# A transformer block with attention and expert choice: the first tiles reordered, the first expert's tokens in two halves

## The chip, the core and the metric

The kernel runs on one NeuronCore of a Trainium2 chip. The core has five engines with their own instruction streams: TensorE (PE: matrix products, results in PSUM), VectorE (DVE), ScalarE (ACT), GpSimd (POOL) and SyncE (SP, which here only issues DMAs). An engine works through its own stream in order and waits for others by semaphores. The metric is the device time of one execution in microseconds (us); smaller is better.

## The reference

One block on x of 8 batches with 1024 tokens of 256 numbers each, all in float32. First attention with 16 heads of 64, then a feed-forward layer in which each of 8 experts chooses its 512 best tokens of all 8192:

```python
mod = (silu(c) @ wmod).reshape(8, 6, 1, 256)      # sa, ca, ga, sb, cb, gb
h = layernorm(x) * (1 + ca) + sa
x = x + ga * attention(h, w_qkv, w_o)             # 16 heads, softmax over 1024 keys
h = layernorm(x) * (1 + cb) + sb
scores = softmax(h @ router_w + router_b)
G, idx = top_k(scores.T, 512)                     # per expert
h1 = relu(h[idx] @ w1 + b1)                       # 256 -> 1024
eo = h1 @ w2 + b2                                 # 1024 -> 256
y = zeros.at[idx].add(eo * G)
x = x + gb * y
```

(ga and gb are kept at least 0.25 away from zero.)

## The kernel before

**Order.** Everything of note lies under a manual schedule: what the Python code emits first stands first in its engine's stream. Tiles, banks of PSUM and semaphores are managed by the framework: an instruction waits until what it reads is written, and until the buffer that it writes is free.

**Beginning.** `first_loads` queues the loads on SP: part of wmod, x of batch 0 as four tiles `x_first` of 256 tokens (tiles 0 and 1; then the k and q weights of the first four heads, in this order; then tiles 2 and 3), then the v weights. `mod_silu` and `mod_columns` make modT (shift and 1 + scale, by columns); its two copies out of PSUM are VectorE's (L218, L219). For each tile, `ln_first` takes mean and variance (L116, L117, VectorE), `ln_norm` has GpSimd make 1/std (`rstd_of`, L106 and L108) and VectorE normalize in place (L288), and `ln_out` turns the tile by four transposes into one PSUM bank (L301) and evicts it to hT with modT as scale and bias, both of its halves k=0 and k=1 on ScalarE (L305). The order is: statistics 0, statistics 1, norm 0, modT, statistics 2, norm 1, statistics 3, norm 2, norm 3.

**Attention.** The loop over g follows. A unit u is one batch, one pair of heads and 512 queries; it takes four steps of g, each with two tiles of 128 keys. A step multiplies scores (L375), copies them to SBUF (L384, ScalarE) and takes the running maximum (L389, VectorE); the maximum is then subtracted (L437, VectorE), exp taken (L440, ScalarE), the values multiplied (L450) and the sums of exp added up on GpSimd (L470, L473). Other work is put between by hand: `at(g, where, f, ...)` appends f to a list that step g runs at its place "m1", "m2", "load", "post" or "pool". Step -1 runs before all scores. There stand `ln_out` of tiles 0 and 1, then `qk_task` i=0 (k of tokens 0 to 511) and i=2 (q of the same tokens, L340, evicted by L347 and L345). Step 0 runs two tiles of scores, then `ln_out` of tiles 2 and 3, then `qk_task` i=1 (k of tokens 512 to 1023). Step 1 has the next scores, `qk_task` i=3, and the first `v_task`. Banks of PSUM for this early work come from the list `early`, one bank each in the order of use.

**Output and router.** `out_proj` and what follows put each batch's tokens, with their expert scores, into a table rows_d in DRAM; the last batch is done after the loop. A search on VectorE and TensorE finds each expert's threshold, and a scan gives each chosen token its slot, split into lo (5 bits) and hi.

**Experts.** `entries(e)` builds one-hot matrices on VectorE: hot (32 wide, L1132), at_hi (16 wide, L1137), and ids, which is at_hi times the token number's two parts (L1142, L1145). `choose(e)` multiplies them (L1156), `gather(e)` folds the result to 512 token numbers and has GpSimd gather the rows, 128 per DMA (L1180). `turn(e)` transposes four row tiles twice (k=0, 1; L1193) into two banks and VectorE copies them to xT (L1196). `inner(e, f)`, f=0..7, multiplies by w1 (L1204, three PSUM banks in turn) and ScalarE applies relu with the bias (L1208). `outer(e, j)`, j=0..3, multiplies by w2 (L1216), VectorE adds the bias and multiplies by the gates (L1221, L1222) and GpSimd scatters with addition to the output (L1225), each scatter behind the one before. `entries(e+1)` is emitted ahead of `inner(e)`, `choose(e+1)` and `gather(e+1)` behind its f=4 and f=5, `turn(e+1)` behind `outer(e, 2)`. For expert 0 all of entries, choose, gather and turn lie bare. The last expert runs its inner and outer for two halves of 256 tokens.

Of the kernel before, what the change touches and what calls it, by code (L numbers as in the profile page):

```python
# [28 lines left out]
F32 = mybir.dt.float32  # L29
BF16 = mybir.dt.bfloat16  # L30
# [3 lines left out]
AF = mybir.ActivationFunctionType  # L34
ALU = mybir.AluOpType
# [4 lines left out]
P = 128  # L40
# [4 lines left out]
def adaln_block(  # L45
# [15 lines left out]
    nc = tc.nc  # L61
    B, S, D = x.shape
    H, _, _, N = w_qkv.shape
    E, _, F = w1.shape
    K = 512
# [143 lines left out]
    def mod_columns():  # L209

        pm = ps_av.tile([P, 2 * KC, B], F32, tag="av", name="pm")
        for m in range(2 * KC):
            for k in range(KC):
                nc.tensor.matmul(
                    pm[:, m, :], wm[0][:, k, m * P : (m + 1) * P], sT[:, k, :],
                    start=(k == 0), stop=(k == KC - 1),
                )
        nc.vector.tensor_copy(modT[:, :KC, :], pm[:, :KC, :])  # L218
        nc.vector.tensor_scalar_add(modT[:, KC:, :], pm[:, KC:, :], 1.0)  # L219

    def mod_rows(i):

# [28 lines left out]
    def at(g, where, f, *args):  # L251
        steps.setdefault((g, where), []).append((f, args))
# [40 lines left out]
    def ln_out(b, t):  # L293
        if t == 0:
            hTs[b] = work.tile([P, KC, S], F32, tag="hT", name=f"hT{b}")
        xt = ln_x.pop((b, t))[0]
        pt = bank([P, KC, 2 * P], f"ptx{b}_{t}")
        if b == 0:
            for k in range(KC):
                for i in range(2):  # L300
                    nc.tensor.transpose(  # L301
                        pt[:, k, i * P : (i + 1) * P], xt[:, i, k * P : (k + 1) * P], ident
                    )
            for k in range(KC):
                nc.scalar.activation(  # L305
                    hTs[b][:, k, 2 * t * P : (2 * t + 2) * P], pt[:, k, :], AF.Identity,
                    bias=modT[:, k, b : b + 1], scale=modT[:, KC + k, b : b + 1],
                )
# [23 lines left out]
    def qk_task(b, p, i):  # L332
        a, half = (1, i) if i < 2 else (0, i - 2)
        if half == 0:
            qks[b, p, a] = work.tile([P, S], F32, tag="qk"[a], name=f"qk{a}_{b}_{p}")
        pq = bank([P, 512], f"pq{b}_{p}_{i}")
        sl = slice(half * 512, half * 512 + 512)
        for k in range(KC):
            for m in range(2):
                nc.tensor.matmul(  # L340
                    pq[m * N : (m + 1) * N, :], wq_of(k, a, 2 * p + m), hTs[b][:, k, sl],
                    start=(k == 0), stop=(k == KC - 1),
                )
        if a == 0:
            nc.scalar.mul(qks[b, p, a][:, sl], pq, scale)  # L345
        else:
            nc.scalar.copy(qks[b, p, a][:, sl], pq)  # L347

# [382 lines left out]


    for t in range(NT // 2):
        at(-1 if t < 2 else 0, "m1", ln_out, 0, t)
        ln_task(1, t, free_slot(39 + 4 * t, True))
    for i, g in ((0, -1), (2, -1), (1, 0), (3, 1)):
        at(g, "m1", qk_task, 0, 0, i)
    for t, g in enumerate((1, 2, 3)):
        at(g, "m1", v_task, 0, 0, t)
    for b in range(B):  # L740
# [48 lines left out]
    with tc.manual_schedule():  # L789
# [4 lines left out]
        ln_first(1)  # L794
        ln_norm(0, 0)
        mod_columns()
        for t in range(2, NT // 2):
            ln_first(t)
            ln_norm(0, t - 1)
        ln_norm(0, NT // 2 - 1)  # L800
        for t in parts_of:
            nc.vector.memset(t, 0.0)
        g = -1
# [96 lines left out]
        def turn(t):  # L900
            out_turn(ps_m, b, t, tag="mm")
# [226 lines left out]
    def entries(e):  # L1128


        hot = ew.tile([P, KT, C, LO], BF16, tag="hot", name=f"hot{e}")
        nc.vector.tensor_tensor(  # L1132
            hot, iota_lo.unsqueeze(1).unsqueeze(1).to_broadcast([P, KT, C, LO]),
            lo[:, :, e, :].unsqueeze(3).to_broadcast([P, KT, C, LO]), ALU.is_equal,
        )
        at_hi = ew.tile([P, KT, C, HI], BF16, tag="at_hi", name=f"at_hi{e}")
        nc.vector.tensor_tensor(  # L1137
            at_hi, hi[:, :, e, :].unsqueeze(3).to_broadcast([P, KT, C, HI]),
            iota_hi.unsqueeze(1).unsqueeze(1).to_broadcast([P, KT, C, HI]), ALU.is_equal,
        )  # L1140
        ids = ew.tile([P, KT, C, 2 * HI], BF16, tag="ids", name=f"ids{e}")
        nc.vector.tensor_tensor(  # L1142
            ids[:, :, :, :HI], at_hi, first.unsqueeze(3).to_broadcast([P, KT, C, HI]), ALU.mult
        )
        nc.vector.tensor_scalar(ids[:, :, :, HI:], at_hi, part, None, op0=ALU.mult)  # L1145
        chosen[e] = hot, ids

    def choose(e):
# [35 lines left out]
            rows.append(row)  # L1184
        chosen[e] = tok, rows

    def turn(e):
        tok, rows = chosen[e]
        xT = ew.tile([P, KC, K], F32, tag="xT", name=f"xT{e}")
        for k in range(KC):  # L1190
            px = ps_x.tile([P, K], F32, tag="px", name=f"px{e}_{k}")
            for j in range(KT):
                nc.tensor.transpose(  # L1193
                    px[:, j * P : (j + 1) * P], rows[j][:, k * P : (k + 1) * P], ident
                )
            nc.vector.tensor_copy(xT[:, k, :], px)  # L1196
        h1 = ew.tile([P, FC, K], F32, tag="h1", name=f"h1_{e}")
        chosen[e] = tok, rows, xT, h1

    def inner(e, f, t0=0, n=K):  # L1200
        tok, rows, xT, h1 = chosen[e]
# [31 lines left out]
    with tc.manual_schedule():  # L1233
        entries(0)
        choose(0)
        gather(0)
        turn(0)
        for e in range(E - 1):
            entries(e + 1)
            for f in range(FC):  # L1240
                inner(e, f)
                if f == FC // 2:
                    choose(e + 1)
                if f == FC // 2 + 1:
# [12 lines left out]


# [29 lines left out]
```

## Time and profile before

| What | Value |
|---|---|
| Median of 3 runs (lowest, highest) | 3532.61 us (3531.13, 3533.65) |
| The profiled execution's own time | 3532.22 us |
| Its span, first to last instruction | 3530.5 us |
| Mean granted TensorE clock | 0.989 |
| Busy share: PE, DVE, ACT, POOL | 98%, 79%, 69%, 75% |
| First projections of q and k begin | 12.82 us |
| First scores begin | 19.70 us |
| First expert's one-hots begin | 3266.87 us |
| First expert's w1 matmuls begin | 3283.59 us |
| Second expert's w1 matmuls begin | 3315.37 us |

A row of the timeline has start and duration in us, engine, line, operation, the tile written and the tiles read, the shapes and a count; in brackets stands the idle time of the engine before it and what ended it. "128*64" ahead of a shape is the part of TensorE's array in use. A float32 product is two instructions in the rows, and two products on the halves of the array run beside each other. Times given below for single instructions within a row come from the same trace.

### The profile page before, as it was taken

The numbers are of one execution on the slowest core, as the hardware profiler recorded it, in microseconds if no ns is written. First come the engines' busy times: TensorE is split into PE (matmuls) and PEld (weight loads), VectorE is DVE, ScalarE is ACT, GpSimd is POOL, SyncE is SP. The second block draws the span as 40 slices with busy tenths as digits, with TensorE's granted clock in tenths as the row PEclk, the third lists the DMA queues.
The fourth block names the chain that finished last, engine by engine and source line by source line (L and its number), as shares of the span: only waits on it lengthen the run. The fifth ranks groups of instructions, "written<-read, shape, count | busy, mean of one in ns | idle before, by whom it ended". The sixth has DMA issues, their size and how long they took to land. (4 is left out here: it accounts for less than half of the span.)

```text
span 3530.5 us, 54857 instructions
## 1 busy us (share of the span) xinstructions
PE 3444.8 (98%) x20991; PEld 1454.9 (41%) x20991; DVE 2796.1 (79%) x3507; ACT 2438.1 (69%) x2998; POOL 2664.6 (75%) x1555
## 2 busy tenths in 40 slices
PE   8999999999999999999999999999999999996898
PEld 3333334334433434344333444334333434334566
DVE  6888888888888888888888888888888888886332
ACT  5887877777777777777777777777778777770111
POOL 3788777978788887978788887988788887882233
PEclk9999999999999999999999999999999999997899
DMA  4020012111211112111211112111221112124342
GB/s 79 13 43 31 25 46 62 29 40 46 63 48 36 49 54 57 34 40 46 64 48 36 45 58 57 34 40 46 62 50 33 47 58 54 40 77 145 96 103 43
DMA packets 184091, 183.34 MB, mean 52 GB/s; under 512 B 49148, under 2 KB 161292, under 8 KB 183700
## 3 DMA queue, kind: packets, MB, share of 16 engines
q1 hardware_dynamic: 167860, 158.44, 16.1%
q0 software_dynamic: 7168, 12.72, 1.8%
q10 hardware_dynamic: 8800, 8.68, 0.8%
q8 instruction: 165, 2.70, 0.3%
q14 instruction: 98, 0.80, 0.1%
HBM read 126.01 MB, written 62.16 MB: 53 GB/s over the span
## 5 line engine op out<-in xcount | busy, mean ns | idle before, releaser
L473 POOL TENSOR_TENSOR acc<-acc,p 128x1024 f32<-128x1024 f32 x764 | 1811.7, 2371 | 351.9 <-ACT p L440 318.6
L384 ACT COPY p<-s 128x1024 f32<-128x1024 f32 x1024 | 994.6, 1018 | 401.9 <-PE s L375 390.6
L437 DVE TENSOR_TENSOR p<-p,less 128x1024 f32<-128x1024 f32 x1024 | 1205.8, 1209 | 28.5 <-PE less L434 25.8
L389 DVE TENSOR_TENSOR top<-top,s 128x1024 f32<-128x1024 f32 x768 | 936.2, 1219 | 269.1 <-ACT p L384 228.1
L440 ACT ACTIVATE p<-p 128x1024 f32<-128x1024 f32 x1024 | 1041.6, 1057 | 73.4 <-DVE p L437 72.5
L375 PE MATMUL s<-qk,qk 64*128 64x512 f32 x4096 | 1020.3, 611 | 15.0 <-DVE parts L415 12.0
L450 PE MATMUL av<-p,v 128*64 128x512 f32 x4096 | 970.0, 593 | 1.6 <-ACT p L440 1.6
L375 PEld LDWEIGHTS s<-qk,qk 64*128 64x128 f32 x4096 | 359.2, 186 | 512.4 <-issue 221.5
L340 PE MATMUL pq<-hT,wq 128*64 128x512 f32 x2048 | 498.0, 607 | 2.2 <-ACT hT L305 2.2
L450 PEld LDWEIGHTS av<-p,v 128*64 128x64 f32 x4096 | 279.3, 137 | 457.4 <-issue 353.5
L470 POOL TENSOR_TENSOR acc<-p,p 128x1024 f32<-128x1024 f32 x128 | 304.0, 2375 | 163.9 <-ACT p L440 163.9
L340 PEld LDWEIGHTS pq<-hT,wq 128*64 128x64 f32 x2048 | 125.1, 136 | 341.5 <-issue 205.5
L357 PE MATMUL pv<-wq,hT 128*64 128x256 f32 x2048 | 249.2, 385 | 0.0
L591 PE MATMUL po<-wo,ot 128*64 128x256 f32 x1792 | 205.7, 382 | 0.0
L357 PEld LDWEIGHTS pv<-wq,hT 128*64 128x64 f32 x2048 | 135.7, 136 | 152.3 <-issue 61.2
L407 DVE TENSOR_REDUCE tt<-tt 128x8 f32<-128x1024 f32 x112 | 138.0, 1232 | 67.4 <-PE tt L396 67.3
L1208 ACT ACTIVATE h<-ph,b_sb 128x512 f32<-128x512 f32 (+1 forms) x72 | 46.1, 640 | 209.0 <-PE ph L1204 209.0
L389 DVE TENSOR_TENSOR top<-p,s 128x1024 f32<-128x1024 f32 x128 | 155.5, 1215 | 12.9 <-ACT p L384 12.9
L396 PEld LDWEIGHTS tt<-ident,top 128*128 128x128 f32 x1024 | 109.6, 140 | 109.7 <-DVE top L389 109.7
L535 POOL TENSOR_TENSOR oT<-oT,rb 128x1024 f32<-128x1024 f32 x63 | 150.9, 2395 | 0.0
L591 PEld LDWEIGHTS po<-wo,ot 128*64 128x64 f32 x1792 | 123.5, 137 | 66.2 <-issue 9.4
L396 PE MATMUL tt<-ident,top 128*128 128x128 f32 x1024 | 139.9, 280 | 4.7 <-DVE top L389 4.6
(194 smaller groups left out, 2247.4 us busy)
## 6 DMA issues: line engine op xcount, KB each, us to landing
rb<-rden_d SPq DMA_DIRECT2D x126, 256.0 KB
oT_d<-oT SPq DMA_DIRECT2D x60, 512.0 KB
ot<-oT_d SPq DMA_DIRECT2D x56, 512.0 KB
rows_d<-gb_d SPq DMA_DIRECT2D x8, 1024.0 KB
w<-in_L_ffn_w_dram SPq DMA_DIRECT2D x8, 1024.0 KB
w<-in_L_ffn_w_dram ACTq DMA_DIRECT2D x8, 1024.0 KB
rows_d<-row SPq DMA_DIRECT2D x62, 132.0 KB
lnx<-in_L_attn_inputs_dram SPq DMA_DIRECT2D x28, 256.0 KB
```

Source lines behind the costliest of these rows:

```text
L340: nc.tensor.matmul(pq[m * N : (m + 1) * N, :], wq_of(k, a, 2 * p + m), hTs[b][:, k, sl], start=(k == 0), stop=(k == KC - 1),)
L357: nc.tensor.matmul(pv[m * N : (m + 1) * N, i, :], hTs[b][:, k, t0 : t0 + N], wq_of(k, 2, 4 * g, 4), start=(k == 0), stop=(k == KC - 1),)
L375: nc.tensor.matmul(ps[:, j, :], kt[r, c * P : (c + 1) * P], qt[r, h * QB : (h + 1) * QB], start=True, stop=True,)
L384: nc.scalar.copy(probs[u, c], ps)
L389: nc.vector.tensor_tensor(tops[u], probs[u, 0] if c == 1 else tops[u], ps, ALU.max)
L396: nc.tensor.transpose(turned[u][:, 4 * j + t, :], top[:, j, t * P : (t + 1) * P], ident)
L437: nc.vector.tensor_tensor(probs[u, c], probs[u, c], less[u], ALU.add)
L440: nc.scalar.activation(probs[u, c], probs[u, c], AF.Exp)
L450: nc.tensor.matmul(avs[u][j * N : (j + 1) * N, :], v[:, c, hh * N : (hh + 1) * N], pT[:, j, :], start=(c == 0), stop=(c == NT - 1),)
L470: nc.gpsimd.tensor_tensor(sums[u], pts[0], pts[1], ALU.add)
L473: nc.gpsimd.tensor_tensor(sums[u], sums[u], pt, ALU.add)
L591: nc.tensor.matmul(po[m * N : (m + 1) * N, :], ot[:, p, m * N : (m + 1) * N], wo[:, p, :], start=(p == 0), stop=(p == NP - 1),)
```

## The change

Five edits. (1) modT's two copies are ScalarE's. (2) `ln_out` of batch 0 evicts k=0 on ScalarE and k=1 on VectorE. (3) The beginning's order: norm 1 and the turning of tiles 0 and 1 come ahead of the statistics of tile 2; q is projected ahead of k; tiles 2 and 3 are turned in step -1 behind these projections, and no longer in step 0 behind the first scores. k of the first projection is evicted in two pieces, of 128 and 384 columns. (4) `entries` builds the wide hot last, and the last multiplication for ids is ScalarE's. (5) Expert 0 turns and multiplies its first 256 tokens ahead of the other 256, whose turn stands behind f=4 of the first half; `entries(1)` stands behind the first half's turn, `choose(1)` and `gather(1)` in the second half, and its outer behind both. The last expert's halves, until now written out behind the loop, are emitted by the same loop in the same order.

```diff
@@ -215,8 +215,8 @@
                     pm[:, m, :], wm[0][:, k, m * P : (m + 1) * P], sT[:, k, :],
                     start=(k == 0), stop=(k == KC - 1),
                 )
-        nc.vector.tensor_copy(modT[:, :KC, :], pm[:, :KC, :])
-        nc.vector.tensor_scalar_add(modT[:, KC:, :], pm[:, KC:, :], 1.0)
+        nc.scalar.copy(modT[:, :KC, :], pm[:, :KC, :])
+        nc.scalar.activation(modT[:, KC:, :], pm[:, KC:, :], AF.Identity, bias=ones[:, :1])
 
     def mod_rows(i):
 
@@ -301,11 +301,15 @@
                     nc.tensor.transpose(
                         pt[:, k, i * P : (i + 1) * P], xt[:, i, k * P : (k + 1) * P], ident
                     )
-            for k in range(KC):
-                nc.scalar.activation(
-                    hTs[b][:, k, 2 * t * P : (2 * t + 2) * P], pt[:, k, :], AF.Identity,
-                    bias=modT[:, k, b : b + 1], scale=modT[:, KC + k, b : b + 1],
-                )
+            nc.scalar.activation(
+                hTs[b][:, 0, 2 * t * P : (2 * t + 2) * P], pt[:, 0, :], AF.Identity,
+                bias=modT[:, 0, b : b + 1], scale=modT[:, KC, b : b + 1],
+            )
+            nc.vector.tensor_scalar(
+                hTs[b][:, 1, 2 * t * P : (2 * t + 2) * P], pt[:, 1, :],
+                modT[:, KC + 1, b : b + 1], modT[:, 1, b : b + 1],
+                op0=ALU.mult, op1=ALU.add,
+            )
             return
         for k in range(KC):
             for i in range(2):
@@ -343,6 +347,10 @@
                 )
         if a == 0:
             nc.scalar.mul(qks[b, p, a][:, sl], pq, scale)
+        elif (b, p, half) == (0, 0, 0):
+
+            for s in (slice(0, P), slice(P, 512)):
+                nc.scalar.copy(qks[b, p, a][:, s], pq[:, s])
         else:
             nc.scalar.copy(qks[b, p, a][:, sl], pq)
 
@@ -731,10 +739,11 @@
 
 
     for t in range(NT // 2):
-        at(-1 if t < 2 else 0, "m1", ln_out, 0, t)
         ln_task(1, t, free_slot(39 + 4 * t, True))
-    for i, g in ((0, -1), (2, -1), (1, 0), (3, 1)):
+    for i, g in ((2, -1), (0, -1), (1, 0), (3, 1)):
         at(g, "m1", qk_task, 0, 0, i)
+    for t in range(2, NT // 2):
+        at(-1, "m1", ln_out, 0, t)
     for t, g in enumerate((1, 2, 3)):
         at(g, "m1", v_task, 0, 0, t)
     for b in range(B):
@@ -794,10 +803,12 @@
         ln_first(1)
         ln_norm(0, 0)
         mod_columns()
+        ln_norm(0, 1)
+        ln_out(0, 0)
+        ln_out(0, 1)
         for t in range(2, NT // 2):
             ln_first(t)
-            ln_norm(0, t - 1)
-        ln_norm(0, NT // 2 - 1)
+            ln_norm(0, t)
         for t in parts_of:
             nc.vector.memset(t, 0.0)
         g = -1
@@ -1128,21 +1139,21 @@
     def entries(e):
 
 
+        at_hi = ew.tile([P, KT, C, HI], BF16, tag="at_hi", name=f"at_hi{e}")
+        nc.vector.tensor_tensor(
+            at_hi, hi[:, :, e, :].unsqueeze(3).to_broadcast([P, KT, C, HI]),
+            iota_hi.unsqueeze(1).unsqueeze(1).to_broadcast([P, KT, C, HI]), ALU.is_equal,
+        )
+        ids = ew.tile([P, KT, C, 2 * HI], BF16, tag="ids", name=f"ids{e}")
+        nc.vector.tensor_tensor(
+            ids[:, :, :, :HI], at_hi, first.unsqueeze(3).to_broadcast([P, KT, C, HI]), ALU.mult
+        )
+        nc.scalar.mul(ids[:, :, :, HI:], at_hi, part)
         hot = ew.tile([P, KT, C, LO], BF16, tag="hot", name=f"hot{e}")
         nc.vector.tensor_tensor(
             hot, iota_lo.unsqueeze(1).unsqueeze(1).to_broadcast([P, KT, C, LO]),
             lo[:, :, e, :].unsqueeze(3).to_broadcast([P, KT, C, LO]), ALU.is_equal,
         )
-        at_hi = ew.tile([P, KT, C, HI], BF16, tag="at_hi", name=f"at_hi{e}")
-        nc.vector.tensor_tensor(
-            at_hi, hi[:, :, e, :].unsqueeze(3).to_broadcast([P, KT, C, HI]),
-            iota_hi.unsqueeze(1).unsqueeze(1).to_broadcast([P, KT, C, HI]), ALU.is_equal,
-        )
-        ids = ew.tile([P, KT, C, 2 * HI], BF16, tag="ids", name=f"ids{e}")
-        nc.vector.tensor_tensor(
-            ids[:, :, :, :HI], at_hi, first.unsqueeze(3).to_broadcast([P, KT, C, HI]), ALU.mult
-        )
-        nc.vector.tensor_scalar(ids[:, :, :, HI:], at_hi, part, None, op0=ALU.mult)
         chosen[e] = hot, ids
 
     def choose(e):
@@ -1184,18 +1195,20 @@
             rows.append(row)
         chosen[e] = tok, rows
 
-    def turn(e):
-        tok, rows = chosen[e]
-        xT = ew.tile([P, KC, K], F32, tag="xT", name=f"xT{e}")
+    def turn(e, t0=0, n=K):
+        if t0 == 0:
+            xT = ew.tile([P, KC, K], F32, tag="xT", name=f"xT{e}")
+            h1 = ew.tile([P, FC, K], F32, tag="h1", name=f"h1_{e}")
+            chosen[e] += xT, h1
+        tok, rows, xT, h1 = chosen[e]
         for k in range(KC):
-            px = ps_x.tile([P, K], F32, tag="px", name=f"px{e}_{k}")
-            for j in range(KT):
+            px = ps_x.tile([P, n], F32, tag="px", name=f"px{e}_{k}_{t0}")
+            for j in range(n // P):
                 nc.tensor.transpose(
-                    px[:, j * P : (j + 1) * P], rows[j][:, k * P : (k + 1) * P], ident
+                    px[:, j * P : (j + 1) * P],
+                    rows[t0 // P + j][:, k * P : (k + 1) * P], ident,
                 )
-            nc.vector.tensor_copy(xT[:, k, :], px)
-        h1 = ew.tile([P, FC, K], F32, tag="h1", name=f"h1_{e}")
-        chosen[e] = tok, rows, xT, h1
+            nc.vector.tensor_copy(xT[:, k, t0 : t0 + n], px)
 
     def inner(e, f, t0=0, n=K):
         tok, rows, xT, h1 = chosen[e]
@@ -1234,26 +1247,29 @@
         entries(0)
         choose(0)
         gather(0)
-        turn(0)
-        for e in range(E - 1):
-            entries(e + 1)
-            for f in range(FC):
-                inner(e, f)
-                if f == FC // 2:
-                    choose(e + 1)
-                if f == FC // 2 + 1:
-                    gather(e + 1)
-            for j in range(KT):
-                outer(e, j)
-                if j == 2:
-                    turn(e + 1)
+        for e in range(E):
+            n = K // 2 if e in (0, E - 1) else K
+            if e == 0:
+                turn(0, 0, n)
+            if e + 1 < E:
+                entries(e + 1)
+            for t0 in range(0, K, n):
+                for f in range(FC):
+                    inner(e, f, t0, n)
+                    if e == 0 and t0 == 0 and f == FC // 2:
+                        turn(0, n, n)
+                    if t0 + n == K and e + 1 < E:
+                        if f == FC // 2:
+                            choose(e + 1)
+                        if f == FC // 2 + 1:
+                            gather(e + 1)
+                if e == E - 1 or t0 + n == K:
+                    for j in range(t0 // P if e == E - 1 else 0, (t0 + n) // P):
+                        outer(e, j)
+                        if e + 1 < E and j == 2:
+                            turn(e + 1)
             if e + 4 < E:
                 load_expert(e + 4)
-        for i in range(2):
-            for f in range(FC):
-                inner(E - 1, f, i * K // 2, K // 2)
-            for j in range(KT // 2):
-                outer(E - 1, i * KT // 2 + j)
 
 
 # ---- launch: one core; inputs and outputs as the reference has them ----
```

More of the change, by code (lines that the diff above doesn't have):

```diff
@@ L1128, in entries @@
     def entries(e):
[L1131 to L1134, printed above, removed]
-        )
         at_hi = ew.tile([P, KT, C, HI], BF16, tag="at_hi", name=f"at_hi{e}")
@@ L1144, in entries @@
         )
-        nc.vector.tensor_scalar(ids[:, :, :, HI:], at_hi, part, None, op0=ALU.mult)
+        nc.scalar.mul(ids[:, :, :, HI:], at_hi, part)
+        hot = ew.tile([P, KT, C, LO], BF16, tag="hot", name=f"hot{e}")
+        nc.vector.tensor_tensor(
+            hot, iota_lo.unsqueeze(1).unsqueeze(1).to_broadcast([P, KT, C, LO]),
+            lo[:, :, e, :].unsqueeze(3).to_broadcast([P, KT, C, LO]), ALU.is_equal,
+        )
         chosen[e] = hot, ids
```

## The prediction

> **What bounds the kernel now.** I read four views in this order: the page, the timeline of the first 30 us, the timeline around the first expert, and the waits of the last expert. The page says where time can be saved at all:
>
> ```profile
> span 3530.5 us, 54857 instructions
> PE 3444.8 (98%) x20991; PEld 1454.9 (41%) x20991; DVE 2796.1 (79%) x3507; ACT 2438.1 (69%) x2998; POOL 2664.6 (75%) x1555
> PE   8999999999999999999999999999999999996898
> PEclk9999999999999999999999999999999999997899
> ```
>
> TensorE is busy 98% of the span; only the first slice and the slices 37 and 38 of 40 fall below 9, and there the clock falls too. The change touches just these places, the beginning and the router with the first expert. What is gained there must be carried through some 3200 us of attention and seven experts in which TensorE doesn't wait. Those run relative to TensorE and not to the clock on the wall, so I let a gain pass through whole.
>
> The timeline of the beginning, TensorE's rows and two others (start, duration, in brackets the idle time before and what ended it):
>
> ```profile
> 8.28 1.23 PE L301 MATMUL ptx<-ident,x_first 128*128 128x128 f32 x4
> 10.50 0.70 DVE L288 TENSOR_SCALAR x_first<-x_first,mv_a,rs_a 128x256 f32<-128x256 f32 x2
> 10.94 1.23 PE L301 MATMUL ptx<-ident,x_first 128*128 128x128 f32 x4 [1.44 <-DVE x_first L288]
> 12.20 1.02 ACT L305 ACTIVATE hT<-ptx,modT 128x256 f32<-128x256 f32 x2 [1.65 <-PE ptx L301]
> 12.82 6.17 PE L340 MATMUL pq<-hT,wq 128*64 128x512 f32 x16 [0.65 <-ACT hT L305]
> 19.70 1.99 PE L375 MATMUL s<-qk,qk 64*128 64x512 f32 x8 [0.70 <-ACT qk L345]
> 21.61 1.09 PE L301 MATMUL ptx<-ident,x_first 128*128 128x128 f32 x8
> 24.23 1.94 PE L340 MATMUL pq<-hT,wq 128*64 128x512 f32 x8 [1.52 <-ACT hT L305]
> 26.10 1.13 PE L375 MATMUL s<-qk,qk 64*128 64x512 f32 x4
> ```
>
> Read the brackets: TensorE idles 1.44 (a norm is late), 0.65 (an eviction), 0.70 (q's eviction) and 1.52 us (ScalarE copies two score tiles before four evictions). From 26.10 it runs without such gaps. Also 16 matmuls of L340 take 6.17 us but 8 take 1.94: TensorE starts at half speed. The granted clock's column shows 1.00 here, having no earlier record; the spacing of pairs, 0.85 us up to 17.97 and 0.43 after, tells it.
>
> The first expert, timeline of VectorE and TensorE:
>
> ```profile
> 3266.87 2.29 DVE L1132 TENSOR_TENSOR hot<-iota_lo,lo 128x2048 bf16<-128x2048 f32 x1
> 3269.08 1.22 DVE L1137 TENSOR_TENSOR at_hi<-hi,iota_hi 128x1024 bf16<-128x1024 int32 x1
> 3270.33 1.22 DVE L1142 TENSOR_TENSOR ids<-at_hi,first 128x1024 bf16<-128x1024 bf16 x1
> 3271.47 0.48 DVE L1145 TENSOR_SCALAR ids<-at_hi,part 128x1024 bf16<-128x1024 bf16 x1
> ...
> 3278.12 0.48 PE L1193 MATMUL px<-ident,erow 128*128 128x128 f32 x1 [4.87 <-DMA erow<-rows_d,tok]
> 3279.61 0.47 PE L1193 MATMUL px<-ident,erow 128*128 128x128 f32 x1 [1.02 <-DMA erow<-rows_d,tok]
> 3281.15 0.47 PE L1193 MATMUL px<-ident,erow 128*128 128x128 f32 x1 [1.06 <-DMA erow<-rows_d,tok]
> 3282.29 1.33 PE L1193 MATMUL px<-ident,erow 128*128 128x128 f32 x5 [0.67 <-DMA erow<-rows_d,tok]
> 3283.59 6.67 PE L1204 MATMUL ph<-xT,w 128*128 128x512 f32 x10
> ```
>
> The four one-hot operations run one after another, then each transpose waits for its gathered rows; the last set lands 2.7 us after the second. In the stretches by windows the clock is 0.50 until 3287 and 1.00 from 3288. In the last expert three scatters still follow each other, so its shape stays and only moves.
>
> **The beginning, part by part.** Norm 1 now stands before the statistics of tile 2. It needs POOL's rs, done at 8.84, so its two halves (0.70, from L288) run 8.87 to 9.58 instead of 10.50 to 11.20. Transposes end 0.96 after that (11.20 to 12.17 in the rows): 10.54. The k=0 eviction stays on ScalarE (0.04 wait, 0.56, 0.05 to TensorE, by the single instructions at 12.20): projections start at 11.19 instead of 12.82, **-1.63**. The k=1 eviction on VectorE lies beside it: no such row, so between 0.40 (L288, from SBUF) and 0.42 (L1221, from PSUM); I take 0.42, and it ends before ScalarE's 0.56. Without that cover ScalarE would need 0.46 more for it. modT on ScalarE: two operations of 16 columns, 0.18 each (L204), from 8.45 to at most 9.0; the eviction waits for the transposes until 9.54, so nothing; uncovered it would cost 0.4. Weights: q now comes first, whose weights are queued second, but tile 2, queued behind both, was in use at 9.42; nothing.
>
> The projections take 6.17 again if the clock opens as late after their start as before: end 17.36. Behind them now stand the eight transposes of tiles 2 and 3. VectorE, in its new order: evictions to 10.96, statistics 1.17, POOL 1.2, norm 0.70, the same again: tile 3 is normed at about 17.1, 0.3 before it is due. That is the thin cover of this part; if the clock opens earlier, TensorE waits up to 0.3 here. Eight transposes 1.03 (max_turn's eight in the attention take that). In this time ScalarE evicts k in two pieces: 128 and 384 columns, not in the trace, between 0.18 (16 columns) and 0.59 (512 columns): 0.28 and 0.48, done 0.75 after the projections' end. Scores then start at 17.36+1.02=18.38, run 1.91, and k's second half follows at once with 1.87 (24.23 to 26.10), as its evictions are done a us before. The next scores start at 18.38+1.91+1.87=22.16 instead of 26.10: **-3.94**, of which 2.3 comes from tiles 2 and 3. The second bank for these scores comes free at 22.7 (two copies 1.93, then 1.22 of maximum) and is due at 23.0: covered by 0.3. No DMA changes its queue; SP issues as before, POOL's two later rs have nothing behind them.
>
> **The router's end.** VectorE's chain becomes at_hi 1.22, ids 1.22, hot 2.28; the fourth (0.48) goes to ScalarE, beside hot. With starts 0.03 apart where dependent, the chain ends at 3271.54 instead of 3271.95: **-0.41**. Here a rule speaks against it: the Trainium skill, page "ScalarE: Activation LUTs", section "Rules for kernel authors", wants multiplications on VectorE. By its prices (0.186 + 0.093 for the pointer + 1024 x 0.833 ns) the operation takes an estimated 1.13 us, where the row has 0.48 on VectorE. The nearest ScalarE row (1.02 for 1024 f32 columns) agrees with the estimate. It is over 2 us before hot is done, so the sum stays -0.41; were it in the path it would be +0.65 instead.
>
> **The first expert in halves.** Rows land 0.41 earlier. The transposes of the first two: last one issued at 3279.69, the copy of k=0 (256 columns: 0.42 as L1221) ends at 3280.16, the matmuls start at 3280.21 instead of 3283.59: **-3.38**, the 0.41 in it. Given back: four transposes inside the stream at 0.11 (eight took 0.87 at 3311.04) +0.44, and two streams of 256 columns (6.91 each in the last expert) for 32 of 0.429: +0.10. **Net -2.84.** The second turn waits on VectorE behind entries(1): 3280.6 plus 4.7 is 3285.3; it is due after the fifth f, at 3286.7 with the clock opening as before. Its rows have landed by 3281.9. Its four copies have three more f, 2.6 us, to end in. The gather of expert 1 moves with the stream: it has 12 us of cover.
>
> **The other entries.** For seven experts ScalarE's new multiplication stands ahead of the eight relus and waits for at_hi. In expert 1: at_hi ends at 3317.65, multiplication to 3318.8, first relu to 3319.5 (now 3317.98). TensorE has three banks and needs the first again at 3320.5. Nothing, with 1.0 us of cover each. hot ends 0.4 earlier and is due 2.5 us later: nothing.
>
> **Sum.** Own time of the profiled execution 3532.22 (span 3530.50 and 1.72 around it): -3.94 -2.84 = -6.78 gives 3525.4. The median of the runs lies 0.39 above that execution, so **3525.8**. About 0.2% (7.07 us, a time of 3525.54) is what a measurement of this kernel can tell from no change; the forecast is just short of it.
>
> **The clock, weighed.** The rows show 5.1 and 4.3 us of half speed after a dense start; half of that is lost, 4.7 together. The Trainium skill ("TensorE: Matmul & The Clock Gate", Part 1) has a free-running window of 3.4 us, so the delay should differ per execution. Taking the rows again, the terms cancel; by the page a start with 3.4 us both times would take off another 1.3, with 6.8 add 2.1. The same page's Part 4 denies that transposes count as activity; were they and the small matmuls of L214 to count, the now unbroken row from 4.86 to 10.54 could open the clock before the projections, another -2.5. I take the rows for the forecast, these ends for the range.
>
> **Rivals.**
> - The clock opens earlier (chance 0.19): more connected work ahead of the projections speaks for it, the cold stretch at 3281 to 3283 against it. About 3524.2.
> - The halves save nothing (0.12): the first half stays cold longer, or the second turn waits for VectorE. For it: only 1.4 us between 3285.3 and 3286.7. Against: those copies have three more f. Only the beginning is left: 3532.6-3.9=3528.7.
> - The beginning's gain is swallowed (0.08): VectorE and ScalarE set the pace in the first units, or tile 3's norm comes late. Against: no gap of TensorE from 26.10 to 46. 3532.6-2.8=3529.8.
> - Slower (0.05): the multiplication on ScalarE holds up the relus. Its place is the start of experts 0 to 6, its cover 1.0 us. It costs from 2.1 us of duration on; to pass the bound upward it must add 13.8 us in seven, 2.0 each, so last 4.1 us. Its strided bf16 output is unseen here; the 1.02 row speaks against. It would give 3540.
>
> **How the numbers follow.** The forecast case has 0.56, alone 3524.6 to 3527.2 (clock either way, 0.3 us of thin covers). Two fifths of it lies below 3525.5, with most of the clock case: faster 0.42. Slower 0.05, the rest same 0.53. The range reaches from 3523.7 (clock case) to 3529.0 (the halves case) and leaves out the swallowed case, the slower one and the tail of the clock: 0.17.
>
> **What will show it.** Right: L340's first row at about 11.2; the eight L301 directly behind it with no ScalarE wait after; the third score matmul near 22.2; L1204 from 3276.3 (3280.2 less 3.9), second turn without idle time; eight L1145 on ScalarE near 1.1 us. Wrong: idle time ahead of L301 of tiles 2, 3 or of L1204's second half, pairs of L340 at 0.85 us beyond 18, relus of later experts more than 3 us behind their matmuls, or a shift at 30 us that is gone at 3200.

## The result and the profile after

The changed kernel (the joined kernel, below) takes 3526.06 us (median of 20 runs, 3525.53 to 3527.35), the kernel before 3532.00 us (20 runs, 3530.75 to 3533.65). The ratio is 0.9984 with a 95% interval of 0.9977 to 0.9991: 5.9 us less. The profiled executions, 3532.22 and 3525.67 us, lie 6.55 apart. The page of the changed kernel:

```profile
span 3523.9 us, 54933 instructions
PE 3442.8 (98%) x21023; PEld 1462.3 (41%) x21023; DVE 2796.6 (79%) x3503; ACT 2445.9 (69%) x3013; POOL 2667.6 (76%) x1555
PE   9999999999999999999999999999999999996898
```

The first slice of TensorE now has a 9; the rest is as it was, moved. The timeline of the beginning, TensorE first, then ScalarE and VectorE:

```profile
11.20 5.03 PE L344 MATMUL pq<-hT,wq 128*64 128x512 f32 x16 [0.65 <-ACT hT L304]
16.16 0.65 PE L301 MATMUL ptx<-ident,x_first 128*128 128x128 f32 x4
17.31 0.82 PE L301 MATMUL ptx<-ident,x_first 128*128 128x128 f32 x4 [0.50 <-ACT qk L353]
18.06 1.99 PE L383 MATMUL s<-qk,qk 64*128 64x512 f32 x8
19.98 1.94 PE L344 MATMUL pq<-hT,wq 128*64 128x512 f32 x8
21.85 1.99 PE L383 MATMUL s<-qk,qk 64*128 64x512 f32 x8
...
9.58 0.56 ACT L304 ACTIVATE hT<-ptx,modT 128x256 f32<-128x256 f32 x1 [0.81 <-PE ptx L301]
10.58 0.56 ACT L304 ACTIVATE hT<-ptx,modT 128x256 f32<-128x256 f32 x1 [0.44 <-PE ptx L301]
...
10.18 0.54 DVE L308 TENSOR_SCALAR hT<-ptx,modT 128x256 f32<-128x256 f32 x1 [0.59 <-ACT hT L304]
11.18 0.55 DVE L308 TENSOR_SCALAR hT<-ptx,modT 128x256 f32<-128x256 f32 x1 [0.46 <-ACT hT L304]
11.64 0.42 DVE L116 BATCH_NORM_STATS2 st_a<-x_first 128x6 f32<-128x256 f32 x1
16.80 0.73 DVE L288 TENSOR_SCALAR x_first<-x_first,mv_a,rs_a 128x256 f32<-128x256 f32 x2 [1.09 <-POOL rs_a L108]
```

The projections start at 11.20 (12.82 before), the second pair of score tiles at 21.85 (26.10). Three things differ from the forecast. Sixteen matmuls took 5.03 instead of 6.17, since the clock opened 2.8 us after their start (5.1 before); by "opened" I mean that the granted clock in the trace's record went from 0.50 to 1.00. VectorE's evictions begin only when ScalarE's of the same tile are over. And so tile 3's norm, 16.80 to 17.53, is late: TensorE waits 0.50 ahead of L301 at 17.31 (the row names ScalarE, but what ended at 17.2 is the norm's first half).

The first expert, two rows of the kernel before and then the joined kernel:

```profile
3266.42 0.42 DVE L1116 TENSOR_SCALAR hi<-slot 128x512 int32<-128x512 int32 x1
3304.34 0.42 DVE L1221 TENSOR_TENSOR eo<-peo,b_sb 128x256 f32<-128x256 f32 x1 [6.89 <-PE peo L1216]
```

```profile
3262.70 0.42 DVE L1127 TENSOR_SCALAR hi<-slot 128x512 int32<-128x512 int32 x1
3263.16 1.23 DVE L1143 TENSOR_TENSOR at_hi<-hi,iota_hi 128x1024 bf16<-128x1024 int32 x1
3264.42 1.22 DVE L1148 TENSOR_TENSOR ids<-at_hi,first 128x1024 bf16<-128x1024 bf16 x1
3265.56 2.29 DVE L1153 TENSOR_TENSOR hot<-iota_lo,lo 128x2048 bf16<-128x2048 f32 x1
...
3267.99 0.69 PE L1167 MATMUL pi<-ids,hot 128*32 128x32 bf16 x64 [6.39 <-DVE hot L1153]
3275.68 0.90 PE L1207 MATMUL px<-ident,erow 128*128 128x128 f32 x3 [1.13 <-DMA erow<-rows_d,tok]
3276.73 6.45 PE L1217 MATMUL ph<-xT,w 128*128 128x256 f32 x20
3283.01 0.60 PE L1207 MATMUL px<-ident,erow 128*128 128x128 f32 x4
3283.45 7.07 PE L1217 MATMUL ph<-xT,w 128*128 128x256 f32 x32
...
3297.74 0.42 DVE L1234 TENSOR_TENSOR eo<-peo,b_sb 128x256 f32<-128x256 f32 x1 [5.18 <-PE peo L1229]
```

Measured from the start of hi, the last step of the split (3266.42 before, 3262.70 now), the w1 matmuls start after 14.03 instead of 17.17 us, and VectorE's first product row (L1221 before, L1234 now) comes after 35.04 instead of 37.92: -2.88. The second half's transposes at 3283.01 have no idle time ahead of them.

### The profile page after: what moved, and what is told of

Its sections match the earlier page's. It is cut to its first block, busy times and chain, and to the rows that moved or that the text cites. A ratio compares the mean times of both kernels' runs of the same rounds, so it can differ in the third digit from the quotient of the medians.

```text
span 3523.9 us, 54933 instructions
## 1 busy us (share of the span) xinstructions
PE 3442.8 (98%) x21023; PEld 1462.3 (41%) x21023; DVE 2796.6 (79%) x3503; ACT 2445.9 (69%) x3013; POOL 2667.6 (76%) x1555
## 5 line engine op out<-in xcount | busy, mean ns | idle before, releaser
L349 ACT ACTIVATE qk<-pq 128x512 f32<-128x512 f32 x128 | 76.5, 598 | 96.3 <-PE pq L344 96.3
```

## The experiments

Five of the kernels ran once (e1_banks 3526.76, e5_mul_vector 3526.09, e8_step0 3527.23, e9_k_whole 3526.67, e10_tiles 3527.85 us); of these the traces are read and not the times.

**Each place alone.** The beginning's edits with the experts of before, and the reverse:

```
e3_begin:   the joined kernel's code up to entries(), from there on the code of before
e4_experts: the code of before up to entries(), from there on the joined kernel's
```

> The beginning's edits alone; router and experts as before. My theory (two independent gains, each carried through): the second pair of score tiles starts near 21.9 us (26.10 before, 21.85 in the joined kernel), the first expert's w1 matmuls start about 3.7 us earlier than before, and the median falls by 3.3 to 4.0 us against the kernel before, some 2.5 more than in the joined kernel. Rival (the beginning's gain is swallowed in the attention or at the router): the marks at 22 us move, but the first expert's one-hots start less than 1 us earlier, and the median falls by less than 1 us.

> The one-hots' new order and the first expert in halves alone; the beginning as before. My theory: everything up to the router stands as before, the first w1 matmuls start 3.2 us earlier against the end of the split into lo and hi, the second expert's w1 matmuls 2.9 us earlier, and the median falls by 2.5 to 3.0 us. Rival (the halves save nothing, what is won at the start is given back in the stream): the second expert's start moves by less than 1 us.

Medians 3528.59 (ratio 0.9990, interval 0.9984 to 0.9997) and 3529.27 (0.9993, 0.9984 to 1.0001), against 3531.65 before: 3.1 and 2.4 us, 5.4 together. Both are under what I expected (3.3 to 4.0 and 2.5 to 3.0), but they add up, within what the medians can tell, to the joined 5.9. The interval of e4_experts alone reaches 1; its gain is read from the trace. Measured from hi to VectorE's first product row, e4_experts has 34.31 and e3_begin 36.92 us; the expert's clock opened 2.7 and 2.4 us after the dense start. So the halves and the one-hots bring 2.6 us, or 2.8 for a like opening (half of 0.3 added). The last expert, now emitted by the common loop, takes as long as before: 21.60 us from expert 6's first product row to its own.

Two parts were not tried alone, modT's copies on ScalarE and q ahead of k. By the rows the first is worth next to nothing: in the joined kernel VectorE idles 0.33 us ahead of norm 1, waiting for GpSimd, and that is where the two copies (0.17 each) would stand.

In the traces of e4_experts and e2_scalar (below), taken together, ScalarE's copies of like score tiles are 3.79 us apart at 26 us and still 3.75 at 2970: the attention carries the gain. Behind that point some 0.3 us are lost, in the joined kernel between 3121 and 3126, where one maximum of VectorE begins 0.4 us after its semaphore instruction instead of 0.05. All twelve traces with the new beginning lose 0.27 to 0.36 between 2970 and 3132; the two with the old one don't. The cause stays open.

**VectorE's share of the evictions.**

```diff
+            if t < 2:
+                nc.scalar.activation(
+                    hTs[b][:, 1, 2 * t * P : (2 * t + 2) * P], pt[:, 1, :], AF.Identity,
+                    bias=modT[:, 1, b : b + 1], scale=modT[:, KC + 1, b : b + 1],
+                )
+                return
             nc.vector.tensor_scalar(
                 hTs[b][:, 1, 2 * t * P : (2 * t + 2) * P], pt[:, 1, :],
```

> The joined kernel with the k=1 eviction of tiles 0 and 1 on ScalarE again. In the joined kernel VectorE's evictions began only when ScalarE's of the same tile had ended (10.18 after 10.14, 11.18 after 11.14), so that they ran one after another, and the statistics of tile 2 began at 11.64. My theory: VectorE's share of that edit saves nothing and holds VectorE up; without it the projections start at 11.2 all the same, the statistics of tile 2 start near 9.7, tile 3 is normed before 16.2 instead of at 17.5, TensorE's wait of 0.5 us ahead of tile 3's transposes is gone, and the second pair of score tiles starts 0.5 earlier where the clock opens as early as there (at the same time where it opens a us or more later). Rival (two engines share the evictions with profit): ScalarE's evictions of tile 1 end 0.5 later and the projections start at 11.6 or later.

```profile
16.67 1.09 PE L301 MATMUL ptx<-ident,x_first 128*128 128x128 f32 x8
17.70 1.99 PE L389 MATMUL s<-qk,qk 64*128 64x512 f32 x8
21.48 1.99 PE L389 MATMUL s<-qk,qk 64*128 64x512 f32 x8
...
9.53 0.42 DVE L116 BATCH_NORM_STATS2 st_a<-x_first 128x6 f32<-128x256 f32 x1
14.68 0.73 DVE L288 TENSOR_SCALAR x_first<-x_first,mv_a,rs_a 128x256 f32<-128x256 f32 x2 [1.09 <-POOL rs_a L108]
```

Tile 3 is normed 2.1 us earlier, its eight transposes run without a wait, and the projections start at 11.22 all the same. The comparison is best with the joined kernel's second profile (j_joined, further down), where the clock opened at the same 15.0: its projections start 0.21 later, its eight transposes take 1.58 instead of 1.09, and its second pair starts at 22.09, so 0.40 is the worth of the edit. In the median it can't be seen (3526.27 us). So VectorE's share saved nothing and cost up to half a microsecond: ScalarE's second eviction of tile 0 ends at 10.62, just as the transposes of tile 1 do (10.57).

Why do the evictions not run beside each other? First with two banks:

```diff
-        pt = bank([P, KC, 2 * P], f"ptx{b}_{t}")
+        pt = bank([P, KC, 512 if b == 0 and t < 2 else 2 * P], f"ptx{b}_{t}")[:, :, : 2 * P]
```

> The joined kernel with the halves k=0 and k=1 of tiles 0 and 1 turned into two banks of PSUM instead of one. My theory: the two evictions ran one after another because both read one bank; in two banks VectorE's begins within 0.05 us of the transposes' end, at about 9.62 and 10.60 instead of 10.18 and 11.18, the statistics of tile 2 begin at about 11.0. Rival (they are ordered because both write hT, or because VectorE's needs modT from ScalarE): still 10.18 and 11.18.

```profile
9.65 0.56 ACT L304 ACTIVATE hT<-ptx,modT 128x256 f32<-128x256 f32 x1 [0.83 <-PE ptx L301]
...
10.25 0.54 DVE L308 TENSOR_SCALAR hT<-ptx,modT 128x256 f32<-128x256 f32 x1 [0.33 <-ACT hT L304]
11.51 0.54 DVE L308 TENSOR_SCALAR hT<-ptx,modT 128x256 f32<-128x256 f32 x1 [0.72 <-ACT hT L304]
```

My theory fell: in two banks they still follow each other, the second pair too (ScalarE's ended at 11.48). So a tile of its own for each half:

```diff
+        if b == 0 and t < 2:
+            pts = [bank([P, 2 * P], f"ptx{b}_{t}_{k}") for k in range(KC)]
...
+            nc.scalar.activation(
+                hTs[b][:, 0, 2 * t * P : (2 * t + 2) * P], pts[0], AF.Identity,
...
+            nc.vector.tensor_scalar(
+                hTs[b][:, 1, 2 * t * P : (2 * t + 2) * P], pts[1],
...
```

> The joined kernel with the two halves k=0 and k=1 of tiles 0 and 1 turned into two PSUM tiles of their own, one bank each. In e1_banks two banks of one tile were still read one after the other. My theory: the order comes from the tile, which two engines read in turn; with a tile for each half VectorE's evictions begin within 0.1 us of ScalarE's, the statistics of tile 2 at about 11.1 instead of 11.64, and the projections at 11.2 all the same. Rival (the order comes from hT, which both write): VectorE still begins 0.6 us after ScalarE.

```profile
8.93 0.56 ACT L304 ACTIVATE hT<-ptx,modT 128x256 f32<-128x256 f32 x1 [0.35 <-PE ptx L301]
9.93 0.56 ACT L304 ACTIVATE hT<-ptx,modT 128x256 f32<-128x256 f32 x1 [0.44 <-PE ptx L301]
...
9.36 0.54 DVE L308 TENSOR_SCALAR hT<-ptx,modT 128x256 f32<-128x256 f32 x1
10.36 0.54 DVE L308 TENSOR_SCALAR hT<-ptx,modT 128x256 f32<-128x256 f32 x1 [0.45 <-PE ptx L301]
10.82 0.42 DVE L116 BATCH_NORM_STATS2 st_a<-x_first 128x6 f32<-128x256 f32 x1
```

Now VectorE waits for TensorE and no longer for ScalarE, and works beside it for 0.13 us (9.36 to 9.49; k=1 is transposed last): in separate banks, the order belongs to the PSUM tile, whose readers take turns. It comes from the program, not from a limit of the engines. The Trainium skill ("PSUM — Partial Sum Buffer", "PSUM bank collisions raise a hardware error") says that two engines may not use one bank on the same partitions at once, reads included. That would forbid the joined kernel's pair in any case, though no run here lets two engines meet in a bank; the two banks of e1_banks were kept apart beyond it.

The statistics of tile 2 begin at 10.82 instead of 11.64. Yet the wait ahead of tile 3's transposes stays, 0.51 us, since the projections end 0.8 earlier too (15.40). Two more effects were not expected. ScalarE waits for two transposes instead of four: from norm 1 to the projections it is 1.93 us (8.62 to 10.55) instead of 2.35. And TensorE idles 2.26 us near 44 us, ahead of the modulation's rows: I had renamed the banks of `early` for the two new tiles, and these rows now come to the bank that the maximum's values hold. VectorE's last use of these ends at 44.35, and the rows start at 44.45.

**The place of tiles 2 and 3, and k in two pieces.**

```diff
+    for t in range(2, NT // 2):
+        at(0, "m1", ln_out, 0, t)
     for i, g in ((2, -1), (0, -1), (1, 0), (3, 1)):
         at(g, "m1", qk_task, 0, 0, i)
-    for t in range(2, NT // 2):
-        at(-1, "m1", ln_out, 0, t)
```

> The joined kernel with tiles 2 and 3 turned in step 0 again, behind the first two score tiles. My theory: their place is worth 2.3 us at a given end of the first projections: the second pair of score tiles starts 7.1 us after that end (joined kernel 5.6, of which 0.5 is the wait for tile 3's norm), with an idle time of 1 to 1.5 us of TensorE ahead of k's second half, ended by ScalarE's or VectorE's eviction. Rival (VectorE's share of the evictions removes that idle time by itself): 5.6 us or less.

```profile
17.26 1.99 PE L383 MATMUL s<-qk,qk 64*128 64x512 f32 x8 [0.37 <-ACT qk L353]
...
21.34 1.08 PE L344 MATMUL pq<-hT,wq 128*64 128x512 f32 x4 [1.07 <-ACT hT L304]
22.58 1.08 PE L344 MATMUL pq<-hT,wq 128*64 128x512 f32 x4 [0.16 <-DVE hT L308]
23.59 1.99 PE L383 MATMUL s<-qk,qk 64*128 64x512 f32 x8
```

The second pair starts 6.7 us after the projections' end (16.90); 7.1 was expected, as before. Two idle times have come back, 1.23 us together. In the joined kernel the distance is 5.6 and 5.2 (its two profiles), in e2_scalar, without the wait, 4.7. So the new place is worth 1.1 to 1.5 in the joined kernel and 2.0 without the wait, where I expected 2.3. The 1.5 is the better figure: there the clock opened at 15.0, in e8_step0 at 15.2.

```diff
-        elif (b, p, half) == (0, 0, 0):
-            for s in (slice(0, P), slice(P, 512)):
-                nc.scalar.copy(qks[b, p, a][:, s], pq[:, s])
```

> The joined kernel with k of the first projection evicted in one piece. My theory: the two pieces are worth nothing, since eight transposes stand between the projection and the scores; the scores start as long after the projections' end as in the joined kernel (1.8 us with a wait for tile 3, 1.0 without one). Rival (the split is in the path): 0.3 us or more later.

Scores start 1.11 us after the projections' end (16.95 to 18.06), in e2_scalar 0.96, in the joined kernel 1.83 and 1.44: the two pieces are worth nothing here. The distance falls with the clock's delay, 1.83, 1.44, 1.34 (e1_banks) for delays of 2.8, 3.6, 3.8 us, and e9_k_whole, with 1.11 for 4.3, lies on that line. With tiles 2 and 3 behind the scores they probably would be worth some 0.3: the wait of 0.37 in e8_step0 was 0.70 in the kernel before. No run has k whole there.

**The one-hots.** The multiplication back on VectorE:

```diff
-        nc.scalar.mul(ids[:, :, :, HI:], at_hi, part)
+        nc.vector.tensor_scalar(ids[:, :, :, HI:], at_hi, part, None, op0=ALU.mult)
```

> The joined kernel with the last multiplication for ids back on VectorE, between ids' first half and hot. My theory: VectorE's chain for expert 0 is longer by one operation of 0.48, of which 0.08 overlaps: from the end of the split into lo and hi to the one-hot matmuls 5.3 us instead of 4.87 (5.17 in the kernel before), so the multiplication on ScalarE is worth some 0.4 us; the first relu of experts 1 to 6 comes 0.7 to 1.5 us earlier with nothing gained. Rival (ScalarE's part is not hidden, since it needs 1.15 us): 4.9 us or less.

From the start of hi to the one-hot matmuls: 5.59 us before, 5.29 joined, 5.68 here (the expected numbers count from its end, 0.42 later). ScalarE's part is worth 0.39; the order by itself costs 0.09 (with the multiplication on VectorE), since with hot last TensorE begins 0.14 instead of 0.06 after VectorE's end. The second expert's first relu begins 1.92 us after its w1 matmuls instead of 3.37, with nothing gained.

Now hot ahead again, with the multiplication on ScalarE (the hot block moved above at_hi):

> The joined kernel with hot ahead of at_hi and ids again; the multiplication stays on ScalarE, ahead of the relus. It tests the slower rival of the prediction, a multiplication that holds up the relus for more than about 1.0 us. at_hi is then done 2.2 us later, and the multiplication with it. My theory: in experts 1 to 6 the first relu ends near 6.3 us after the first w1 matmul instead of 4.1; TensorE needs that bank after 5.2 us and waits 1.1 us in each; expert 0 loses about as much. In all 6 to 8 us, a time near 3533; for expert 0 alone the one-hot matmuls start 0.1 us earlier. So the order, the wide one last, is worth this and not the 0.4 of the first chain. Rival (the order doesn't matter, TensorE is covered by its banks): no wait within w1's matmuls, the time as that of the joined kernel.

3534.42 us (ten runs, 3533.89 to 3534.89; ratio to the kernel before 1.0007, 0.9997 to 1.0017): 8.4 more than the joined kernel's 3526.06, and all that the change gains is gone. The expected 0.1 us in the first chain did not come: 5.29 us from hi to the one-hot matmuls, as joined. The timelines of experts 0 and 1, TensorE and ScalarE:

```profile
3282.61 1.99 PE L1217 MATMUL ph<-xT,w 128*128 128x256 f32 x8 [0.51 <-ACT h L1221]
3310.21 5.31 PE L1217 MATMUL ph<-xT,w 128*128 128x512 f32 x12
3316.50 3.70 PE L1217 MATMUL ph<-xT,w 128*128 128x512 f32 x8 [0.98 <-ACT h L1221]
...
3314.72 1.15 ACT L1156 ACTIVATE ids<-at_hi,part 128x1024 bf16<-128x1024 bf16 x1 [18.53 <-DVE at_hi L1148]
3315.78 1.82 ACT L1221 ACTIVATE h<-ph,b_sb 128x512 f32<-128x512 f32 x3
```

After twelve matmuls (three f) the banks are full; TensorE waits for the first relu, which stands behind the multiplication, which waits for at_hi. In the joined kernel's second expert the same chain stands like this, and TensorE runs through:

```profile
3308.78 8.75 PE L1217 MATMUL ph<-xT,w 128*128 128x512 f32 x20
...
3311.09 1.15 ACT L1151 ACTIVATE ids<-at_hi,part 128x1024 bf16<-128x1024 bf16 x1 [16.33 <-DVE at_hi L1143]
3312.15 1.25 ACT L1221 ACTIVATE h<-ph,b_sb 128x512 f32<-128x512 f32 x2
```

From one expert's first product row to the next one's it is 30.81 in e6_hot_first and 29.57 joined, six times over: 7.4 of the 8.4 us. So "the wide one-hot last" doesn't earn its part in the bare chain; it is what makes room for ScalarE's multiplication, so that TensorE is spared the wait of 1.0 us.

**The half speed at both starts.** The joined kernel again as the standard, and one in which TensorE is kept busy with products that nobody reads (four more stand behind the first transpose of turn(0), and k=1 of tiles 0 and 1 is evicted by ScalarE as in e2_scalar):

```diff
+        fill(waste[:, 0, :], idle[:, :P], idle, 2)
         mod_silu()
+        fill(waste[:, 1, :], idle[:, :P], idle, 5)
...
+        fill(waste[:, 0, :], idle[:, :P], idle, 1)
         ln_out(0, 0)
+        fill(waste[:, 1, :], idle[:, :P], idle, 1)
         ln_out(0, 1)
+        fill(waste[:, 0, :], idle[:, :P], idle, 2)
...
         gather(0)
+        waste = ps_h.tile([P, K], F32, tag="ph", name="waste_h")
+        fill(waste, *waste_in, 16)
```

> The joined kernel itself again, unchanged, as the standard for the next one on the same chip. All theories: 3525.5 to 3526.5 us as the median.

> The joined kernel with the k=1 eviction of tiles 0 and 1 on ScalarE (as in e2_scalar) and with TensorE kept busy in its idle time by products whose result nobody reads: eleven of 512 bf16 columns before the first projections, twenty between the one-hot matmuls of expert 0 and its first w1 matmul. My theory: both dense stretches start at half speed because TensorE had too little to do before, 3.8 us each in the mean of the runs so far, half of which is lost; with the filling the clock is open when they start: pairs of the first projections 0.43 us apart from the start (3.7 us for the sixteen instead of 5.0 to 6.2), the first five f of expert 0 in 4.4 us instead of 6.2 to 6.5, the median 2.5 to 3.8 us below the joined kernel's, with a smaller spread. Rival (half speed after the start has another cause, or the gate closes again in the short gaps): spacing 0.85 us at the start of both as before, the median no lower or higher by what the filling delays, up to 1.5 us.

Joined: 3525.95 (20 runs; ratio 0.9983, 0.9976 to 0.9990). Filled: 3523.70 (10 runs, 3523.02 to 3524.97; 0.9976, 0.9967 to 0.9986), 2.2 less where 2.5 to 3.8 was expected, and with no smaller spread (1.95 against 1.61). By windows (stretch, its length, busy time and count of PE, PEld, DVE, ACT, POOL, then the clock) and by the timeline:

```profile
3272.00:3273.00 1.00, 1.00 (x4) 0.43 (x3) 0.00 (x0) 0.00 (x0) 0.69 (x2) 0.50 0.67 221
3273.00:3274.00 1.00, 1.00 (x6) 0.39 (x4) 0.00 (x0) 0.00 (x0) 0.69 (x2) 0.85 0.69 133
3274.00:3276.00 2.00, 1.83 (x11) 0.96 (x9) 0.35 (x2) 0.00 (x0) 0.88 (x1) 1.00 0.74 212
...
3268.59 5.94 PE L806 MATMUL waste_h<-hot 128*128 128x512 bf16 x16
3276.17 4.96 PE L1237 MATMUL ph<-xT,w 128*128 128x256 f32 x20 [0.34 <-issue]
```

The clock opens at 3273.3, ahead of the gathered rows' transposes, and the first five f take 4.96 instead of 6.45 (4.4 expected). For the second place the theory holds. At the beginning it does not: the clock opened at 13.58, after the projections' start, which the filling had delayed to 12.18; the five products from 3.30 to 5.41, 2.1 us in one piece, did not open it. Whether more of them would have, no run shows.

Last, what the runs point to: tiles of their own for both halves, evicted by ScalarE, with the later banks kept, and the filling of expert 0 alone.

```diff
+    early = [(ps_s, "s")] * 2 + [(ps_b, "less"), (ps_av, "av"), (ps_m, "mm"), (ps_av, "av")] + [
...
+            for k in range(KC):
+                pt = bank([P, 2 * P], f"ptx{b}_{t}_{k}")
...
+                nc.scalar.activation(
+                    hTs[b][:, k, 2 * t * P : (2 * t + 2) * P], pt, AF.Identity,
```

> What the runs point to, in one kernel: the joined one with each half of tiles 0 and 1 turned into a PSUM tile of its own and evicted by ScalarE, with the banks of the early work named so that the later ones keep theirs (in e10_tiles the rows of the modulation got the bank of the maximum and cost 2.3 us near 44), and with the twenty filling products of expert 0, but none at the beginning (where e11_fill's came too late by the 1.0 us that they cost). My theory: the projections start at 10.6 to 10.9 instead of 11.2 to 11.4, no wait ahead of tile 3's transposes, no slip at 44; the first five f of expert 0 in 5.0 us; the median 3523.0 to 3523.8, at least 2 us below the joined kernel's 3526.0. Rival (the gains are not added up, since the clock's windows decide): 3524.5 or more.

```profile
10.58 4.43 PE L356 MATMUL pq<-hT,wq 128*64 128x512 f32 x16 [0.23 <-ACT hT L304]
14.94 1.09 PE L313 MATMUL ptx<-ident,x_first 128*128 128x128 f32 x8
3274.70 4.96 PE L1232 MATMUL ph<-xT,w 128*128 128x256 f32 x20 [0.35 <-issue]
```

3523.02 us (seven runs, 3522.18 to 3523.45; ratio 0.9973, 0.9962 to 0.9984), 2.9 below the joined kernel's 3525.95 on another chip, where the kernel before took 0.4 less (3532.39 against 3532.80). The projections start at 10.58, no wait, no slip at 44, and the clock of expert 0 opened at 3271.9. At the beginning it opened 1.6 us after their start, the shortest delay of all kernels without filling there; whether by chance or by the shorter gap ahead of them (0.23 us) stays open. The new tiles with ScalarE alone were not run without the filling.

## Why the prediction was right

The forecast, 3525.8, is 0.3 from the median, and the case (both gains, just inside 0.2%) is what happened. Both gains came by the path that was forecast, and e3_begin and e4_experts show each alone. That the number is so close is in part luck: in the profile the clock opened earlier than assumed at both places, and the starting value was too high. The steps held unequally.

- **Projections 1.63 earlier:** 1.62 measured. But "beside it" failed for the k=1 eviction: it ran behind ScalarE's, to 11.72, and cost nothing only because TensorE starts on k=0 and needs k=1 0.9 us later. I had looked for the operation's price and not for who else reads the tile. The trace of before showed it: each of L389's 896 maxima began after L384's copy of the same score tile had ended (the first at 22.83, after 22.80). The 0.46 that ScalarE would need without this cover was wrong as well: in e2_scalar the projections start at 11.22.
- **Tile 3 "0.3 before it is due":** the thin cover broke. Normed at 17.53 instead of 17.1, due at 16.8: a wait of 0.50, shown by e2_scalar to come from VectorE's share.
- **Second pair at 22.16:** 21.85, two errors of opposite sign, the clock opening 2.3 us earlier after the start (1.1 of time) and the wait with what follows it. At a given clock e2_scalar has 4.74 from the projections' end; the step's 4.80 was right without the wait.
- **Tiles 2 and 3 worth 2.3:** too high; e8_step0 has 1.5 for the joined kernel, and 2.0 against e2_scalar.
- **Whole gain carried:** -4.25 at 22 us, -3.7 at the router. Part is the slip of 0.35 near 3125; the other 0.2 is an even drift over 3000 us between profiles taken at different times, and is nearly absent (0.04) between those taken together.
- **One-hots -0.41:** -0.30; the term left out is TensorE's later start behind hot.
- **Expert 0, -2.84 with the one-hots:** -2.88, by luck: the w1 matmuls start 3.14 earlier and not 3.38, since the second gathered rows came 0.21 and not 0.41 earlier (12.98 us after hi instead of 13.19), and the clock, opening 0.5 us earlier after the start, gave 0.2 back.
- **Relus covered by 1.0 us:** shown by e6_hot_first from the other side. The slower rival's mechanism was real, its place too; what kept it from happening is the place of at_hi, which the forecast used without naming its worth. The multiplication takes 1.15 us, near the estimated 1.13.
- **The sum:** -6.78 forecast, -6.55 between the two profiles, -5.94 between medians of 20. The start, the median of three runs, was 0.6 too high, and this made up for most of the gain that was missing. The clock case did not come to be: in no run did the transposes and small matmuls ahead of the projections open the clock before them.

## What to carry to other kernels

Before an eviction is shared between two engines, look in the trace whether two engines ever read one PSUM tile at the same time; a tile for each reader costs a bank and gives the overlap. Then ask whether it is needed: here one engine alone had the time. When work moves to another engine's stream, count from what it waits for to what stands behind it: the same multiplication was free or cost 8 us, by the order of two lines on a third engine. And where TensorE idles for some microseconds ahead of a dense stretch, products that nobody reads can pay.

## What the runs showed of the hardware

All openings of the clock lie on a grid. From the first to the second opening it is 3269.97 us before and in e10_tiles, 3259.73 in e11_fill and e12_both, and 3266.55 in the ten others: steps of 3.41 or twice that, and each is a whole number of them (958, 955 and 957 times 3.413). This is the window of 3.4 us that the Trainium skill names ("TensorE: Matmul & The Clock Gate", Part 1), and its free run: over the thirteen starts without filling at the beginning the delay was 1.6 to 5.2 us, with a mean of 3.6. What I had not thought of is that both delays of one execution hang together: the kernel all but fixes the distance of its two dense starts, and with the grid the second delay follows from the first, up to whole windows (2.8 and 3.9 us joined, 3.6 and 4.2 in its second profile, 5.1 and 4.3 before). The two can add up or even out, as the distance falls. That this makes the spread of the runs (2.9 us before, 1.8 joined) is argued, not shown.
